# Cross-attention and feed-forward block: the denominators move into the second bank of the tile of the weighted sums

## The chip, the cores and the metric

The kernel runs on one core of one Trainium2 chip. The metric is the device time of one execution in microseconds (us); three runs of the kernel before gave a median of 1290.35 us (1289.89 to 1291.47).

A core has five engines that run beside each other, each with its own queue of instructions that it takes in order: TensorE (PE; its weight loads stand apart as PEld), VectorE (DVE), ScalarE (ACT), GpSimd (POOL) and SyncE (SP), which here issues DMAs. They wait for one another through semaphores. TensorE writes its results to PSUM, where VectorE and ScalarE read them. PSUM has eight banks; a bank holds 512 fp32 numbers in each of 128 partitions.

## The reference

One sequence of 2048 rows of 256 numbers attends to a context of 1601 rows of 192 numbers (and one learned null key and value, so 1602 keys), with 16 heads of 64, and then passes through three layers whose weights are +1 or -1. All in fp32. Cut to what matters:

```python
x = layernorm(x)*g                     # 2048 x 256
q = x @ Wq                             # 16 heads of 64
k, v = split(context @ Wkv); null key and value put in front
sim  = q k^T / 8                       # 2048 x 1602 for each head
attn = softmax(sim)                    # exp(sim - max) / sum
out  = attn @ v                        # the weighted sums, then divided
x = x + layernorm(out @ Wout)*g_out
x = x + three layers(layernorm(x))     # relu between them
```

## The kernel before, in words

**Units.** The attention goes over 32 units `(p, b)`: eight pairs `p` of heads, and for each pair four blocks `b` of 512 rows. The two heads of a pair lie in the two halves of the 128 partitions. The order of all instructions in this part is the order in which the program is written (`manual_schedule`); waits and semaphores are put in by the framework, from what each instruction reads and writes of each tile.

**One unit**, from its scores on, has two stages on TensorE:

- *Scores and the next unit's maxima* (13 steps `k` over the keys, 128 keys each). In step `k` TensorE multiplies keys and queries (`scores`, L391) into one of two tiles `sT`, the even steps into one and the odd steps into the other; ScalarE takes the exponential of it (`exps`, L417) into a tile `e` in SBUF; TensorE then computes one part of the scores of the *next* unit in a cheaper number format (`max_chunk`, L361, and once L345), and VectorE reduces this to maxima (L364, and once L348). In the order of steps L345 with L348 is the last but one and L361 with L364 the last. After the 13 steps VectorE combines the maxima (`max_combined`, L369). GpSimd meanwhile adds the 13 tiles `e` up to `acc` (L665, L667), whose column sums are the denominators of the softmax.
- *Weighted sums.* First the denominators of the *previous* unit: `denominators` (L443) multiplies the previous `acc` by ones with four matmuls on 32 columns of the array each, so that the 512 denominators of each of the two heads stand in 128 partitions by 256 numbers; `divided_quarters` takes the reciprocal of them on VectorE (L455), spreads it with eight copies on ScalarE (L461) and multiplies the previous weighted sums by it on VectorE (L462), which gives `aoT`. Then 13 steps of `weighted` (L424) accumulate values times `e` into bank 0 of the tile `av`; ScalarE copies it to `avs` (L721). After it TensorE transposes the maxima (`max_turned`, L374, read by VectorE in L376), projects the previous unit's `aoT` (`project_out`, L432, added up by VectorE in L437), and makes the queries of the unit after the next (`project_q`, L213) and a part of the next pair's keys or values (`project_k`, `project_v`).

In four units it is otherwise: unit 0 has no previous one, and units 1, 30 and 31 compute the denominators with `divided` (L468) after the third step of the weighted sums. So 28 units go by `denominators` and `divided_quarters`.

**PSUM.** All tiles of PSUM in this part have two banks, `[128, 2, 512]` fp32, and there are four slots of them in two pools of two slots. `flex` gives tiles of the one pool: the tiles of the maxima, `den` (the denominators), `mt` (the transposed maxima), `psq` (queries), and `psk` or `psv` (keys or values). `spare` gives tiles of the other: the two `sT`, `av` and `po` (the projection). A slot is taken over by a new tile when all that read and wrote the old tile is done. `av` uses its bank 0 alone; of a `den` tile 256 numbers of bank 0 are used.

**Two further places** that the prediction looks at. `input_turned` (L491 to L502) transposes the normed input on TensorE: for the blocks 0 and 2 into two PSUM tiles, for block 3 into the two banks of one; ScalarE scales the first half (L498), VectorE the second (L502). `third` (L797 to L825), for the last rows of the third layer, has 32 matmuls (L806), the first sixteen into bank 0 and the others into bank 1 of one tile, and VectorE reads first bank 0 and then bank 1 (L819).

Of the kernel before, what the change touches and what calls it, by code (L numbers as in the profile page):

```python
# [36 lines left out]
def xattn_ffn(ctx, tc, x, ctxT, mask, g_norm, null_kv, wq, wkv, wout, g_out, k0, k1, k2, s0, s1, s2, out):  # L37
# [9 lines left out]
    def flex(name):  # L47
        return ps_f.tile([128, 2, 512], F32, tag="f", name=name)

    def spare(name):  # L50
        return ps_s.tile([128, 2, 512], F32, tag="s", name=name)
# [94 lines left out]
    with ExitStack() as att:  # L146
# [292 lines left out]
        def denominators(acc, ps):  # L439

            for h in range(2):
                for j in range(2):
                    nc.tensor.matmul(  # L443
                        ps[ds(64 * j + 32 * h, 32), :],
                        ones[:, :32],
                        acc[:, j, ts(h, 256)],
                        start=True,
                        stop=True,
                        tile_position=(0, 64 * j + 32 * h),
                    )  # L450

        def divided_quarters(p, b, avs, ps):

            r = lp.tile([128, 256], F32, tag="r", name=f"r_{p}_{b}", bufs=1)
            nc.vector.reciprocal(r, ps)  # L455
            aoT = lp.tile([128, 512], F32, tag="aoT", name=f"aoT_{p}_{b}", bufs=1)

            for j in range(2):
                for h in range(2):
                    for rows in range(2):  # L460
                        nc.scalar.copy(aoT[ds(64 * j + 32 * rows, 32), ts(h, 256)], r[ds(64 * j + 32 * h, 32), :])  # L461
            nc.vector.tensor_tensor(aoT, avs, aoT, ALU.mult)  # L462
            return aoT
# [160 lines left out]
        with tc.manual_schedule():  # L624
            for u, (p, b) in enumerate(units):
# [63 lines left out]


                quarters = last is not None and u not in (1, len(units) - 2, len(units) - 1)
                if quarters:
                    den = flex(f"den_{p}_{b}")[:, 0, :256]
                    denominators(last[3], den)
                    aoT = divided_quarters(*last[:3], den)
                av = spare(f"av_{p}_{b}")
                for k in range(KC):
                    weighted(p, k, es[k], av)
                    if k == 2 and not quarters and last is not None:
# [193 lines left out]
```

## Time and profile before

| | before |
|---|---|
| median of three runs | 1290.35 us |
| span of the profiled execution, first to last instruction | 1288.7 us |
| TensorE busy | 1275.8 us (99%) |
| weight loads on TensorE busy | 648.9 us |
| GpSimd busy | 1001.7 us (78%) |
| VectorE busy | 787.9 us (61%) |
| ScalarE busy | 717.7 us (56%) |
| L391 matmuls of scores, 1664 | 448.5 us |
| L424 matmuls of weighted sums, 1664 | 364.7 us |
| L361 matmuls of maxima, 768 | 276.8 us |
| L443 matmuls of denominators, 224 | 28 groups of 8, 0.64 us each |
| L455 reciprocal, 28 | 1.748 us each |
| mean granted clock of TensorE | 1.000 |

The profile was taken from one execution; its span is what the runs' times are to be compared with. A line of the timeline gives the start and the duration of a group of like instructions in us, its engine and line, what it writes and reads, the shape, and in brackets how long the engine had been idle before it and what ended that. The chain of waits is followed back from the last instruction, at each step to what released it, and so tells which engine and line set the end. Matmuls overlap, and their ends are modelled, so the busy time of TensorE says more of being occupied than of being fast; the distance between starts is the better measure.

### The profile page before, as it was taken

What the parts mean: (1) busy time and instruction counts of PE and PEld (TensorE: products, weight loads), DVE (VectorE), ACT (ScalarE), POOL (GpSimd) and SP (SyncE); (2) the same over time, 40 slices, a digit from 0 to 9 for tenths busy, and PEclk for the clock granted to TensorE, in tenths of its full rate; (3) what the DMA queues carried; (4) which work ended last, traced back from release to release, by engine and by line L of the source; (5) the groups of instructions that cost most, each with busy time, mean ns of one, the idle gap of its engine ahead of it and who ended that gap; (6) DMA issues with size and microseconds to landing.
All of it is one profiled execution on the core that took longest, in us unless ns stands there. A gap on an engine that the chain in (4) does not pass through costs nothing.

```text
span 1288.7 us, 16385 instructions
## 1 busy us (share of the span) xinstructions
PE 1275.8 (99%) x6672; PEld 648.9 (50%) x6672; DVE 787.9 (61%) x817; ACT 717.7 (56%) x965; POOL 1001.7 (78%) x508
## 2 busy tenths in 40 slices
PE   8999999999999999999999999999999999999998
PEld 6334444444444444444444444444444443788887
DVE  7887866655665566556666666666666784644432
ACT  4766556655555555555565666666655667422120
POOL 5798988998889888989899889988998999801100
PEclk9999999999999999999999999999999999999999
DMA  5000000000000000000000000000000010000000
GB/s 145 22 1 5 1 1 13 5 1 1 13 5 2 1 13 5 1 1 13 5 1 1 1 14 5 1 1 5 1 17 1 1 41 1 1 9 9 17 17 17
DMA packets 16156, 13.19 MB, mean 10 GB/s; under 512 B 2688, under 2 KB 15552, under 8 KB 16080
## 3 DMA queue, kind: packets, MB, share of 16 engines
q1 hardware_dynamic: 14944, 11.02, 3.1%
q8 instruction: 52, 0.85, 0.3%
q10 hardware_dynamic: 656, 0.79, 0.2%
q0 software_dynamic: 480, 0.34, 0.2%
q14 instruction: 24, 0.20, 0.1%
HBM read 10.04 MB, written 2.10 MB: 9 GB/s over the span
## 4 chain that ended last, share of the span: by engine, by line
PE 96%; DVE 2%; DMA 1%; ACT 1%; issue 0%; SPq 0%; DVEq 0%; ACTq 0%
PE sT L391 29%; PE av L424 27%; PE ps L775 11%; PE max L361 7%; PE po L432 4%; PE psq L213 4%; PE ps L806 2%; PE psv L303 2%; PE psk L243 1%; PE sT L415 1%; PE den L443 1%; PE psv L315 1%; DMA x_sb<-in_x 1%; PE psk L248 1%; PE max L345 1%; ACT e L417 1%
## 5 line engine op out<-in xcount | busy, mean ns | idle before, releaser
L667 POOL TENSOR_TENSOR acc<-acc,e 128x1024 f32<-128x1024 f32 (+1 forms) x352 | 847.3, 2407 | 27.6
L364 DVE TENSOR_REDUCE mx<-max 128x2 f32<-128x1024 f32 x384 | 450.3, 1220 | 80.3 <-PE max L361 78.4
L417 ACT ACTIVATE e<-sT,maskb 128x1024 f32<-128x1024 f32 (+1 forms) x416 | 460.4, 1113 | 40.4 <-PE sT L391 9.1
L391 PE MATMUL sT<-qT,kT 64*128 64x512 f32 (+1 forms) x1664 | 448.5, 613 | 1.5 <-ACT e L417 0.9
L424 PE MATMUL av<-e,v 128*64 128x512 f32 (+1 forms) x1664 | 364.7, 594 | 0.2 <-ACT e L417 0.2
L361 PE MATMUL max<-kr,qr 64*128 64x512 f32 x768 | 276.8, 712 | 1.9 <-DVE mx L364 1.9
L424 PEld LDWEIGHTS av<-e,v 128*64 128x64 f32 (+1 forms) x1664 | 116.7, 137 | 233.5 <-issue 230.5
L391 PEld LDWEIGHTS sT<-qT,kT 64*128 64x128 f32 (+1 forms) x1664 | 128.2, 181 | 146.6 <-ACT e L417 133.3
L461 ACT COPY aoT<-r 32x256 f32<-32x256 f32 x224 | 90.1, 402 | 63.9 <-DVE r L455 61.6
L361 PEld LDWEIGHTS max<-kr,qr 64*128 64x128 f32 x768 | 75.3, 187 | 95.8 <-DVE mx L364 67.4
L665 POOL TENSOR_TENSOR acc<-e,e 128x1024 f32<-128x1024 f32 x32 | 75.6, 2361 | 61.4 <-ACT seen L655 52.2
L721 ACT COPY avs<-av 128x512 f32<-128x512 f32 x32 | 18.7, 585 | 159.7 <-PE av L424 159.7
L462 DVE TENSOR_TENSOR aoT<-avs,aoT 128x512 f32<-128x512 f32 x28 | 43.1, 1539 | 94.3 <-ACT aoT L461 94.3
L376 DVE TENSOR_TENSOR mT<-mt,pick 128x512 fp32r<-128x512 f32 x32 | 22.1, 689 | 106.9 <-PE mt L374 106.9
L775 PE MATMUL ps<-h0hi,w 128*128 128x512 f32 x256 | 79.5, 392 | 0.0
L775 PE MATMUL ps<-h0lo,w 128*128 128x512 f32 x256 | 78.9, 389 | 0.0
L122 POOL TENSOR_TENSOR y_sb<-y_sb,gout_sb 128x256 f32<-128x256 f32 x12 | 9.3, 775 | 86.7 <-DVE y_sb L89 86.7
L214 ACT ACTIVATE qr<-psq 128x512 fp32r<-128x512 f32 x32 | 19.1, 597 | 97.8 <-PE psq L213 95.1
L763 ACT ACTIVATE h1hi<-ps 128x1024 fp32r<-128x1024 f32 x16 | 16.4, 1026 | 98.9 <-PE ps L775 98.9
L764 DVE SCALAR_TENSOR_TENSOR h1lo<-ps,h1hi 128x1024 fp32r<-128x1024 f32 x16 | 19.6, 1223 | 67.8 <-ACT h1hi L763 67.8
L432 PE MATMUL po<-wo,aoT 128*128 128x256 f32 x256 | 60.6, 379 | 0.0
L213 PE MATMUL psq<-xnT,wq 128*128 128x512 f32 x124 | 58.4, 593 | 0.6 <-ACT xnT L498 0.6
(164 smaller groups left out, 1135.4 us busy)
## 6 DMA issues: line engine op xcount, KB each, us to landing
out_x<-o SPq DMA_DIRECT2D x7, 256.0 KB, 2.2
x_sb<-in_x SPq DMA_DIRECT2D x3, 512.0 KB, 8.2
wa<-in_wkv SPq DMA_DIRECT2D x8, 128.0 KB, 2.7
wq<-in_wq SPq DMA_DIRECT2D x8, 128.0 KB, 2.2
wo<-in_wout SPq DMA_DIRECT2D x8, 128.0 KB, 2.0
xnT<-in_k SPq DMA_DIRECT2D x1, 1024.0 KB, 5.7
wb<-in_wkv SPq DMA_DIRECT2D x15, 64.0 KB, 2.4
ctx_a<-in_ctxT SPq DMA_DIRECT2D x2, 256.0 KB, 8.1
```

Of the source, the lines that this page charges most:

```text
L213: nc.tensor.matmul(ps[:, 0, :], weights[p][0][:, c, :], xnT[:, b, c, :], start=c == 0, stop=c == 1)
L361: nc.tensor.matmul(ps[:, j, :w], qr[rows, ts(t, 128)], kr[rows, ds(start, w)], start=True, stop=True)
L364: nc.vector.tensor_reduce(maxima[p, b][:, t, :, c], ps[:, :, :w], AX.X, ALU.max)
L391: nc.tensor.matmul(ps[:n, j, :], kT[rows, ds(128 * k, n)], qT[rows, :], start=k < 2, stop=k >= 2, skip_group_check=k >= 2,)
L417: nc.scalar.activation(e[:n], ps[:n], AF.Exp, bias=maskb[:n, k : k + 1])
L424: nc.tensor.matmul(av[ts(j, DH), 0, :], v[:n, k, ts(j, DH)], e[:n, j, :], start=k == 0, stop=k == KC - 1)
L432: nc.tensor.matmul(pv[:, t, :], aoT[:, ts(t, 128)], weights[p][3], start=True, stop=True)
L461: nc.scalar.copy(aoT[ds(64 * j + 32 * rows, 32), ts(h, 256)], r[ds(64 * j + 32 * h, 32), :])
L462: nc.vector.tensor_tensor(aoT, avs, aoT, ALU.mult)
L665: nc.gpsimd.tensor_tensor(acc, es[0], es[1], ALU.add)
L667: nc.gpsimd.tensor_tensor(acc[:m], acc[:m], es[k][:m], ALU.add)
L775: nc.tensor.matmul(ps[:, f, :], w(c)[:, ts(2 * g + f, 128)], parts[part][:, c, :], start=i == 0, stop=i == len(steps) - 1,)
```

## The change

The tile `av` is taken from `spare` ahead of the denominators instead of behind them. In the 28 units that go by `denominators`, the four matmuls of L443 write the first 256 numbers of bank 1 of `av`, and the reciprocal (L455) reads them there. No tile `den` is taken from `flex` in these units. Nothing else is changed: the instructions of every engine and their order are as they were, and `divided` in the other units still takes its own tile from `flex`.

```diff
                 quarters = last is not None and u not in (1, len(units) - 2, len(units) - 1)
+                av = spare(f"av_{p}_{b}")
                 if quarters:
-                    den = flex(f"den_{p}_{b}")[:, 0, :256]
+                    den = av[:, 1, :256]
                     denominators(last[3], den)
                     aoT = divided_quarters(*last[:3], den)
-                av = spare(f"av_{p}_{b}")
                 for k in range(KC):
                     weighted(p, k, es[k], av)
                     if k == 2 and not quarters and last is not None:
```

## The prediction

> **What bounds the kernel now.** I read the engines' shares and the chain of waits first, then one unit of the attention loop in order of time, then the list of waits, and last two places far from the change that show how accesses to one PSUM tile are ordered.
>
> ```profile
> span 1288.7 us, 16385 instructions
> ...
> PE 1275.8 (99%) x6672; PEld 648.9 (50%) x6672; DVE 787.9 (61%) x817; ACT 717.7 (56%) x965; POOL 1001.7 (78%) x508
> ...
> PE 96%; DVE 2%; DMA 1%; ACT 1%; issue 0%; SPq 0%; DVEq 0%; ACTq 0%
> ```
>
> TensorE is busy or on the chain nearly throughout: whatever holds it up is paid in full, unless a later wait absorbs it. One unit looks like this at the place of the change (start, duration, engine, line):
>
> ```profile
> 557.41 1.11 ACT L417 ACTIVATE e<-sT,maskb 128x1024 f32<-128x1024 f32 x1
> ...
> 557.77 0.71 DVE L348 TENSOR_REDUCE mx<-max 128x8 f32<-128x528 f32 x1
> ...
> 558.05 0.80 PE L361 MATMUL max<-kr,qr 64*128 64x512 f32 x2
> 558.72 1.11 ACT L417 ACTIVATE e<-sT,maskb 66x1024 f32<-66x1024 f32 x1 [0.20 <-PE sT L391]
> ...
> 558.78 0.64 PE L443 MATMUL den<-acc,ones 128*32 128x256 f32 x8
> 558.89 1.23 DVE L364 TENSOR_REDUCE mx<-max 128x2 f32<-128x1024 f32 x1 [0.41 <-PE max L361]
> ...
> 559.35 3.65 PE L424 MATMUL av<-e,v 128*64 128x512 f32 x16
> ...
> 560.15 0.19 DVE L369 TENSOR_REDUCE mcol<-mx 128x8 f32<-128x32 f32 x1
> 560.25 1.75 DVE L455 RECIPROCAL r<-den 128x256 f32<-128x256 f32 x1
> ```
>
> The weighted sums (L424) start 0.57 us after the denominators (L443), while VectorE has not begun to read these: it first reduces the last maxima (L364) and combines them (L369), and its reciprocal runs from 560.25 to 562.00. Today that reading is off the path, because den has a tile of its own.
>
> **How one PSUM tile is ordered.** The input's transposes stand in two PSUM tiles for block 2 and in the two banks of one tile for block 3. ScalarE reads bank 0 (L498), VectorE bank 1 (L502); everything else is alike.
>
> ```profile
> 64.48 0.69 ACT L498 ACTIVATE xnT<-xT,gn_sb 128x512 f32<-128x512 f32 x1 [0.32 <-PE xT L497]
> 64.58 0.75 DVE L502 TENSOR_SCALAR xnT<-xT,gn_sb 128x512 f32<-128x512 f32 x1 [1.81 <-PE xT L497]
> ...
> 99.92 0.69 ACT L498 ACTIVATE xnT<-xT,gn_sb 128x512 f32<-128x512 f32 x1 [0.43 <-PE xT L497]
> 100.64 0.75 DVE L502 TENSOR_SCALAR xnT<-xT,gn_sb 128x512 f32<-128x512 f32 x1 [2.49 <-ACT xnT L498]
> ```
>
> With two tiles the two reads overlap; with one tile the second starts 0.03 us after the first has ended (100.61), and ACT's L498 is named as its releaser, though the banks differ. The kernel's end says the same of a read behind writes:
>
> ```profile
> 1282.58 0.28 PE L806 MATMUL ps<-w,h1lo 128*128 128x256 f32 x1
> ...
> 1284.50 0.28 PE L806 MATMUL ps<-w,h1lo 128*128 128x256 f32 x1
> 1284.82 0.88 DVE L819 SCALAR_TENSOR_TENSOR o<-ps,s_out,x_sb 128x256 f32<-128x256 f32 x2 [3.08 <-PE ps L806]
> ```
>
> The first L819 reads bank 0 alone, whose sixteen matmuls end with the one at 1282.58 (the next sixteen, 0.12 us apart up to 1284.50, write bank 1). It waits for the last of bank 1, about 2 us too long. So in this program the waits go by tile, not by bank, whatever the chip would allow.
>
> **The change, part by part.**
>
> 1. *den becomes bank 1 of av; the weighted sums write bank 0 of the same tile.* Going by the rows above, the first L424 must now wait for the end of the reciprocal. The instructions on TensorE and VectorE and their order are as before, so the reciprocal cannot move: it follows L364 and L369 in VectorE's queue. It ends at 560.25 + 1.75 = 562.00. A waiting weight load starts about 0.05 us after its releaser's end (the exp that ends at 556.18 is followed by L391's load at 556.23), so L424 starts at 562.05 instead of 559.35: 2.70 us later. Over the 28 units that compute den this way (L455 stands 28 times, and the reciprocal starts 1.47 to 1.48 us after den in each): 28 x 2.70 = **75.6 us**. Bounds: 0, if only the bank counts; 28 x 2.70 otherwise, since neither side of the difference varies by more than 0.01 us.
>
> 2. *What queues behind it.* All 52 L424, then the transpose of the maxima, the projection of the outputs, the next queries and keys or values, and with them the next unit's scores. ScalarE's last exp (to 559.83) and its copies L461 (from 562.03) do not wait for L424; its copy of av (L721) does, and shifts along. Does a later stage absorb it? TensorE's weight loads wait there for exps (133.3 us in all) and for maxima (67.4 us), but these are made in the same stage from scores that shift too: nothing in it was ready early. GpSimd's sums (78% busy) get more room. I take no absorption; at the other end, one that took all would leave 0.
>
> 3. *den's own start.* It waited for the reduction L348 of the tile two back in the rotation (ends 558.48); it will wait for the exp that last read the odd score tile (557.41 + 1.11 = 558.52), from which av takes its slot. That it is this slot is seen today: L424 starts at 559.35, before the other slot's exp ends at 559.83. den started 0.73 us after the last L361 (558.05); in the unit without den, L424 itself starts 0.72 us after its L361 (85.90, 86.62). So TensorE's own finishing and changing over sets this, with some 0.2 us to spare after 558.57: cost 0. Bounds: -15.7 us, all 28 idle times of the weight loads before den; +28 x (559.83 + 0.05 - 558.78) = +31 us, were it the other slot. This overlaps with 1: a later den still ends ahead of the reciprocal's turn unless it passes 560.25, so on top of 75.6 both ends shrink to about nothing.
>
> 4. *The rotation of the maxima is one tile shorter.* The transpose of the maxima takes the slot of the tile read by L348, the queries the slot of the last L364 (read by 560.12) instead of den's. They start at 570.66 and 572.34: more than 10 us of cover, cost 0. The order of all later tiles two apart is unchanged. No DMA and no queue of SP or GpSimd is touched.
>
> Sum: 0 + 75.6 + 0 = 75.6 us on the profiled 1288.7, so a span of 1364.3; the runs' median is 1.65 us above this span: **1366.0 us**.
>
> The Trainium skill ("PSUM — Partial Sum Buffer", section "Summary: rules for kernel authors") speaks for the change: to read PSUM while matmuls run, use another bank and guard by bank. By it the sum would be 0; by the row of L502, 75.6. I go by the row.
>
> **The clock.** Each unit gets a pause of TensorE of 562.05 - 559.42 = 2.63 us, den's end to L424. Two pauses of before enclose it:
>
> ```profile
> 72.90:74.50 1.60, 0.06 (x4) 0.03 (x2) 1.60 (x3) 1.19 (x3) 1.60 (x2) 1.00 0.04 10
> 74.50:78.00 3.50, 3.50 (x20) 1.57 (x20) 3.50 (x4) 2.11 (x2) 3.42 (x2) 1.00 0.00 0
> 1284.80:1287.80 3.00, 0.00 (x0) 0.00 (x0) 0.88 (x2) 0.00 (x0) 0.00 (x0) 1.00 0.26 87
> 1287.90:1288.70 0.80, 0.00 (x0) 0.00 (x0) 0.00 (x0) 0.00 (x0) 0.00 (x0) 0.50 0.00 0
> ```
>
> (columns: length, busy us of PE, PEld, DVE, ACT, POOL, granted clock, DMA.) After 1.54 us without matmuls the clock stayed at 1.00; after the last matmul it still was 1.00 for 3.0 us and then 0.50. At 2.63 us into that idle time it had not fallen, so I take no loss. Upper bound: the run's first matmuls ran at half rate for 5.1 us (24 in 2.70 to 7.80 us, 18 in the 1.9 us from 7.90 on); as much after each pause costs 28 x 5.1 / 2 = 71 us.
>
> The Trainium skill ("TensorE: Matmul & The Clock Gate", section "What's actually happening") has the clock halve after an idle window of about 3.4 us that runs freely; a pause of 2.6 us never fills one, so by it too the loss is 0 unless a mostly idle window counts as idle.
>
> **The rivals.**
> - *Forecast, 0.62:* the wait on the reciprocal at full clock, 1366 (its own range 1362 to 1369).
> - *The wait, and the clock falls in some of the pauses, 0.25:* for it, 2.63 is nearer to 3.0 than to 1.54; against, the clock still stood at 2.63. From 1366 to 1437; with a third of the pauses caught, 1366 + 24 = 1390.
> - *The other side, 0.08:* waits go by bank for a matmul behind a read, which no row of before shows (they show a read behind a read and a read behind writes). Then part 1 is nothing and the time 1290.4. The point that decides is the first L424 of each unit: before or after 562.00 in the unit shown. Were den also freed of all the idle time ahead of it, 1274.7 at the best; 0.01 for that.
> - *Part of the wait is absorbed, 0.04:* for it, 200 us of waits in the stage of the scores; against, part 2. Half absorbed: 1328.
>
> **How the numbers follow.** The likeliest is 1366. The range of 8 in 10 takes all of the forecast and the clock's case up to a third of the pauses: 1362 to 1390; above lies about 0.07, below 0.12. Faster by over 0.2% (what a measurement of this kernel can just tell from none): 0.01; within 0.2%: 0.08; slower: 0.91.
>
> **What would show it.** Right: the list of waits has L424's weight loads behind DVE r L455 some 28 times, 2.6 to 2.7 us each, 75 us in all; L455 still 1.47 us after den; VectorE's L364 and L455 on the chain with some 28 x 3.2 us, 6 to 7%; TensorE at about 93%; a unit 2.70 us longer and the projection later by as much; clock 1.00 at every slice. Wrong: L424 still 0.57 us after den (by bank); slices with a clock below 1.00 and L424 more than 0.43 us apart (clock); den more than 0.73 us behind the last L361 (part 3); a unit longer by less than 2.7 us with L424 late (absorbed).

## The result and the profile after

| | before | after |
|---|---|---|
| median of five runs | 1290.41 us | 1399.28 us |
| span of the profiled execution | 1288.7 us | 1397.6 us |
| mean granted clock of TensorE | 1.000 | 0.974 |
| TensorE busy | 1275.8 us | 1312.0 us |

After takes 1.084 times as long as before (95% interval 1.0829 to 1.0852). The prediction was 1366.0 us with a range of 1362 to 1390: slower, as forecast, but 33 us beyond the forecast and 9 us beyond the range.

The page of after, its engines and its chain of waits by engine:

```profile
span 1397.6 us, 16378 instructions
...
PE 1312.0 (94%) x6672; PEld 657.5 (47%) x6672; DVE 787.1 (56%) x817; ACT 717.3 (51%) x965; POOL 1001.3 (72%) x508
...
PE 91%; DVE 7%; DMA 1%; ACT 1%; issue 0%; SPq 0%; DVEq 0%; ACTq 0%
```

VectorE's share of the chain went from 2 to 7%. The list of waits of after (what waited, for what: us in all, times, longest) names the wait:

```profile
PEld av L424 <- DVE r L455: 87.3, 28, 3.1
...
PE av L424 <- DVE r L455: 73.8, 28, 2.6
```

In before neither line exists. TensorE's matmuls (PE), and not only its weight loads (PEld), stood still 28 times, 73.8 / 28 = 2.64 us each, until the reciprocal was done; the weight loads, which had been idle for longer, 87.3 / 28 = 3.12. The timeline of after at one of these places:

```profile
533.52 0.79 PE L361 MATMUL max<-kr,qr 64*128 64x512 f32 x2
...
534.25 0.64 PE L443 MATMUL av<-acc,ones 128*32 128x256 f32 x8
...
535.72 1.75 DVE L455 RECIPROCAL r<-av 128x256 f32<-128x256 f32 x1
...
537.52 4.06 PE L424 MATMUL av<-e,v 128*64 128x512 f32 x10 [2.64 <-DVE r L455]
```

L443 is still 0.73 us behind L361, the reciprocal still 1.47 us behind L443, and the first L424 is 3.27 us behind L443 instead of 0.57: 2.70 us more, in each of the 28 units between 2.70 and 2.71. That is 28 x 2.706 = 75.8 us. The spans differ by 1397.6 - 1288.7 = 108.9 us, so 33.1 us are something else. The last row hints at it: ten matmuls take 4.06 us, where in before sixteen took 3.65.

The table by windows of after, cut at 459.17 and 534.26 us into pieces of 3.41 us (columns: window, length, busy us of PE, PEld, DVE, ACT and POOL, granted clock, DMA share, GB/s), shows what:

```profile
459.17:462.58 3.41, 1.79 (x16) 0.46 (x14) 2.85 (x5) 2.00 (x2) 3.33 (x2) 1.00 0.00 0
462.58:465.99 3.41, 2.39 (x12) 0.92 (x14) 0.96 (x1) 2.35 (x6) 3.25 (x3) 1.00 0.00 0
534.26:537.67 3.41, 0.77 (x12) 0.29 (x12) 3.08 (x3) 1.22 (x2) 3.25 (x3) 1.00 0.00 0
537.67:541.08 3.41, 3.41 (x10) 0.98 (x10) 0.24 (x1) 3.05 (x8) 3.33 (x2) 0.50 0.00 0
541.08:544.49 3.41, 3.41 (x20) 1.13 (x18) 1.21 (x1) 0.00 (x0) 3.33 (x2) 1.00 0.00 0
```

At 534.26 the window holds the whole pause, TensorE is busy for 0.77 us of it, and in the next window the clock is 0.50 and TensorE begins 10 matmuls instead of 20. At 459.17 the same pause is cut by the window's end, neither window has more than 1.62 us without matmuls, and the clock stays at 1.00.

The whole clock record of after has 21 such stretches at 0.50 in the attention (each is called a fall from here on), each 3.413 us long, and all of them begin and end on one grid of 3.413 us, as if a clock that nothing resets cut time into windows. Ahead of each lies a window with 2.18 us or more without matmuls; the seven pauses that left at most 1.70 us in any one window were not followed by a fall. These are the two windows nearest to each other, each with the one behind it:

```profile
271.43:274.84 3.41, 1.23 (x13) 0.19 (x10) 2.96 (x4) 1.45 (x2) 3.26 (x3) 1.00 0.00 0
274.84:278.26 3.41, 2.95 (x8) 1.00 (x10) 0.40 (x1) 2.89 (x8) 3.33 (x2) 0.50 0.00 0
909.72:913.14 3.41, 1.71 (x16) 0.39 (x12) 2.91 (x4) 1.93 (x2) 3.34 (x2) 1.00 0.00 0
913.14:916.55 3.41, 2.48 (x12) 0.92 (x14) 0.88 (x1) 2.43 (x7) 3.26 (x3) 1.00 0.00 0
```

33.1 / 21 = 1.58 us for a fall, close to the 1.71 that half speed over 3.41 us can cost. In units with a fall the projection (L432) comes 1.4 to 1.7 us later than in units without. The mean clock agrees: 21 x 3.413 x 0.5 / 1397.6 = 0.026 under 1.

The page's row of the clock in 40 slices prints 9 ("90% or more") in every slice, in after as in before: a slice is 35 us long, and one fall takes 5% from it. The prediction wanted to read the clock from these slices; they are too coarse for this, and only the mean clock or short windows show it.

### The profile page after: what moved, and what is told of

It is laid out like the page before. It is cut to its first block, busy times and chain, and to the rows that moved or that the text cites. A ratio compares the mean times of both kernels' runs of the same rounds, so it can differ in the third digit from the quotient of the medians.

```text
span 1397.6 us, 16378 instructions
## 1 busy us (share of the span) xinstructions
PE 1312.0 (94%) x6672; PEld 657.5 (47%) x6672; DVE 787.1 (56%) x817; ACT 717.3 (51%) x965; POOL 1001.3 (72%) x508
## 4 chain that ended last, share of the span: by engine, by line
PE 91%; DVE 7%; DMA 1%; ACT 1%; issue 0%; SPq 0%; DVEq 0%; ACTq 0%
PE av L424 29%; PE sT L391 27%; PE ps L775 10%; PE max L361 6%; PE po L432 4%; PE psq L213 4%; DVE r L455 3%; DVE mx L364 3%; PE ps L806 2%; PE psv L303 1%; PE psk L243 1%; PE sT L415 1%; PE psv L315 1%; DMA x_sb<-in_x 1%; PE psk L248 1%; PE max L345 1%
## 5 line engine op out<-in xcount | busy, mean ns | idle before, releaser
L424 PE MATMUL av<-e,v 128*64 128x512 f32 (+1 forms) x1664 | 399.2, 640 | 74.0 <-DVE r L455 73.8
L424 PEld LDWEIGHTS av<-e,v 128*64 128x64 f32 (+1 forms) x1664 | 124.2, 147 | 336.3 <-issue 245.9
L361 PE MATMUL max<-kr,qr 64*128 64x512 f32 x768 | 277.2, 712 | 2.3 <-DVE mx L364 2.3
L665 POOL TENSOR_TENSOR acc<-e,e 128x1024 f32<-128x1024 f32 x32 | 75.6, 2362 | 91.7 <-ACT seen L655 82.5
L361 PEld LDWEIGHTS max<-kr,qr 64*128 64x128 f32 x768 | 75.5, 187 | 96.0 <-DVE mx L364 68.0
L462 DVE TENSOR_TENSOR aoT<-avs,aoT 128x512 f32<-128x512 f32 x28 | 42.0, 1500 | 94.2 <-ACT aoT L461 94.2
L266 POOL TENSOR_TENSOR kT<-kT 128x256 f32<-128x256 f32 (+1 forms) x48 | 31.8, 662 | 46.9 <-DVE kr L255 43.7
L432 PE MATMUL po<-wo,aoT 128*128 128x256 f32 x256 | 60.6, 379 | 0.0
```

The costliest lines, as they stand in the source:

```text
L361: nc.tensor.matmul(ps[:, j, :w], qr[rows, ts(t, 128)], kr[rows, ds(start, w)], start=True, stop=True)
L424: nc.tensor.matmul(av[ts(j, DH), 0, :], v[:n, k, ts(j, DH)], e[:n, j, :], start=k == 0, stop=k == KC - 1)
L432: nc.tensor.matmul(pv[:, t, :], aoT[:, ts(t, 128)], weights[p][3], start=True, stop=True)
L665: nc.gpsimd.tensor_tensor(acc, es[0], es[1], ALU.add)
```

## The experiments

Times are medians of four to ten runs, each against before on the same chip; e8 has a single run. The headings have the labels (e4 and so on) by which the runs are named further down.

**The pause filled (e4, from after).** Between den and the weighted sums:

```diff
+                    fill = flex(f"fill_{p}_{b}")
+                    for _ in range(3):
+                        nc.tensor.matmul(fill[:, 0, :], ident, es[0][:, 0, :], start=True, stop=True)
```

> The kernel after, with three matmuls on 512 columns (0.86 us each by the 512-column matmuls of L424 and L361 at 0.22 to 0.43 us per half-array pair; an estimate of 2.56 us in all) between den and the weighted sums, whose result nobody reads. They stand in TensorE's pause of 2.63 us and so cost nothing there, and the first L424 still waits for the end of L455, 3.28 us after den. Theory (33 of the 109 us are the clock, which falls to 0.50 for 3.41 us after 21 of the 28 pauses because TensorE has too little to do in them): granted clock 1.000 instead of 0.974, no stretch at 0.50 inside the attention, 1290.4 + 75.8 = 1366 us. Rival (the 33 us are something else that a unit loses behind the wait, and the clock record only goes with it): no faster than after, 1399 us or more.

Measured: 1366.76 us, ratio 1.0596 (1.058 to 1.0612), clock 1.000. The cores' view and the timeline of this kernel:

```profile
core 0: 1364.2 us, clock 1.000
```

```profile
556.07 0.64 PE L443 MATMUL av<-acc,ones 128*32 128x256 f32 x8
...
556.64 2.84 PE L698 MATMUL fill<-e,ident 128*128 128x512 f32 x6
...
557.55 1.75 DVE L455 RECIPROCAL r<-av 128x256 f32<-128x256 f32 x1
...
559.41 1.94 PE L424 MATMUL av<-e,v 128*64 128x512 f32 x8
```

TensorE does more work, L424 starts 0.07 us later than in after (3.34 us behind den), and the kernel is 32.5 us shorter. What the fill changes is that TensorE has no pause; that a tile `fill` is taken from `flex` and a matmul is added has no part in the gain, since e7 below does both and gains nothing. So the 33 us are the clock, and what remains, 1364.2 - 1288.7 = 75.5 us in the spans, is the wait. The theory held, the rival fell.

**One fill matmul instead of three (e6, from after).** `range(1)` in the same edit.

> The kernel after, with one matmul of 512 columns (0.86 us) in TensorE's pause, whose result nobody reads: 2.63 - 0.86 = 1.8 us of the pause are left, in one piece. In after, windows of 3.41 us with at most 1.70 us without matmuls never lowered the clock and those with 2.18 us or more always did; 1.8 us lies between. Theory (a share of a window decides): if the threshold is above 1.8 us, clock 1.000 and 1366 us; if it is at half of a window (1.71 us), only windows that take nearly all of the pause fall, about half of 28, and with 33 us for 21 falls that is 1366 + 22 = 1388 us. Rival (the number of falls does not depend on how long the pause is): 21 falls, 1399 us.

Measured: 1365.01 us, ratio 1.0582 (1.0564 to 1.0599), clock 1.000. The cores' view and the waits of this kernel:

```profile
core 0: 1363.4 us, clock 1.000
```

```profile
PE av L424 <- DVE r L455: 44.3, 28, 1.6
```

The fill took more of the pause than I had reckoned, 1.1 us, so 1.58 us were left, under the 1.70 that had been harmless. No fall in 28 pauses: the number of falls depends on how long the pause is. 1.1 us of fill did as well as 2.8. Here L424 still stands and waits for the reciprocal in all 28 units, and the span is 1363.4 - 1288.7 = 74.7 us over before's: the price of the wait alone, with no fall.

**A short touch in the middle of the pause (e7, from after).**

```diff
+                    if nxt is not None:
+                        fill = flex(f"fill_{p}_{b}")
+                        nc.tensor.matmul(fill[:, 0, :8], ident, mcol[:, :8], start=True, stop=True)
```

> The kernel after, with one short matmul (8 columns) that reads the combined maxima and so stands in the middle of TensorE's pause, where L369 ends (about 1.56 us after den's start): the pause of 2.63 us becomes two, of about 1.0 and 1.6 us, with hardly any work between them. The first L424 still waits for the reciprocal, so 1366 us without any loss of clock. Theory (what counts is how much of a window of 3.41 us TensorE is idle, however it is cut: 2.5 of 3.41 us is over the 2.18 from which the clock of after always fell): granted clock about 0.975 and some 20 stretches at 0.50, 1390 to 1400 us. Rival (what counts is the longest stretch without work; 1.6 us is below the 1.70 at which the clock of after never fell): clock 1.000, 1366 us.

Measured: 1398.65 us, ratio 1.0844 (1.0828 to 1.086), clock 0.976, 20 falls in the attention. Timeline and windows of this kernel at one place:

```profile
532.18 0.64 PE L443 MATMUL av<-acc,ones 128*32 128x256 f32 x8
...
533.88 0.36 PE L699 MATMUL fill<-mcol,ident 128*128 128x8 f32 x2 [1.06 <-DVE mcol L369]
...
535.45 4.92 PE L424 MATMUL av<-e,v 128*64 128x512 f32 x14 [1.21 <-DVE r L455]
```

```profile
532.19:535.60 3.41, 1.14 (x14) 0.59 (x14) 3.08 (x3) 1.22 (x2) 3.25 (x3) 1.00 0.00 0
535.60:539.01 3.41, 3.41 (x10) 0.97 (x10) 0.24 (x1) 3.05 (x8) 3.33 (x2) 0.50 0.00 0
```

Neither of the two idle stretches (1.06 and 1.21 us) is as long as those that did no harm in one piece, and the clock falls all the same. It is the sum of idle time in a window that counts, not the longest stretch: the rival fell. The least idle time ahead of a fall is 1.81 us here, with the touch counted as 0.36 us of work; without it, it would be 2.17, about as in after.

**Half of the reciprocal, first try (e3, from after).**

```diff
-            nc.vector.reciprocal(r, ps)
+            nc.vector.reciprocal(r[:, :128], ps[:, :128])
+            nc.gpsimd.memset(r[:, 128:], 1.0)
```

> The kernel after, where the reciprocal takes 128 of the 256 columns only and the others are set to 1.0 by GpSimd, so half of the denominators are left out. L455 then takes about half of 1.75 us, 0.88. Theory (L424 waits for the end of L455 and for nothing else): first L424 at 1.47 + 0.88 + 0.06 = 2.41 us after den instead of 3.28, so 28 x 1.84 = 51.5 us over before, 1342 us at full clock, and up to 22 us more if half of the pauses, now 1.8 us long, lower the clock. Rival (it waits for something else in VectorE's or ScalarE's queue, such as the copies L461): first L424 still 3.28 us after den, 1366 us or more.

Measured: 1637.24 us, ratio 1.2692 (1.2673 to 1.2711), clock 0.922: more than 270 us above what was expected. The timeline of one unit:

```profile
617.72 26.74 POOL L668 TENSOR_TENSOR acc<-acc,e 128x1024 f32<-128x1024 f32 x11
...
627.19 0.64 PE L443 MATMUL av<-acc,ones 128*32 128x256 f32 x8
...
628.66 0.95 DVE L455 RECIPROCAL r<-av 128x128 f32<-128x128 f32 x1
...
629.66 11.38 PE L424 MATMUL av<-e,v 128*64 128x512 f32 x52 [1.84 <-DVE r L455]
...
644.40 0.20 POOL L456 MEMSET r<- 128x128 f32 x1
644.64 3.29 ACT L462 COPY aoT<-r 32x256 f32<-32x256 f32 x8 [16.40 <-POOL r L456]
```

What was to be measured came out nearly as expected: L424 2.47 us behind den (2.41 expected), after a reciprocal of 0.95 (0.88). But the memset of 0.20 us stands in GpSimd's queue behind the unit's sums (L668), which end at 644.46; the copies L462 need it, wait 16.40 us, and everything behind them is late; with longer pauses of TensorE the clock falls further as well (0.922). I had put a small instruction into the queue that is furthest behind, on the way to something that TensorE needs, and had not asked what stands in front of it.

**Half of the reciprocal, used twice (e3b, from after).**

```diff
-            r = lp.tile([128, 256], F32, tag="r", name=f"r_{p}_{b}", bufs=1)
-            nc.vector.reciprocal(r, ps)
+            r = lp.tile([128, 1, 128], F32, tag="r", name=f"r_{p}_{b}", bufs=1)
+            nc.vector.reciprocal(r[:, 0, :], ps[:, :128])
...
-                        nc.scalar.copy(aoT[ds(64 * j + 32 * rows, 32), ts(h, 256)], r[ds(64 * j + 32 * h, 32), :])
+                        nc.scalar.copy(
+                            aoT[ds(64 * j + 32 * rows, 32), ts(h, 256)].rearrange("p (t q) -> p t q", t=2),
+                            r[ds(64 * j + 32 * h, 32), 0:1, :].to_broadcast([32, 2, 128]),
+                        )
```

> The kernel after, where the reciprocal takes 128 of the 256 columns only and its result is used for both halves, so half of the denominators are left out; nothing is put into GpSimd's queue. Theory (L424 waits for the end of L455 and for nothing else): L455 takes 0.95 us as in the run before, the first L424 comes 1.47 + 0.95 + 0.06 = 2.48 us after den instead of 3.28, so the unit is 1.91 us longer than before's: 28 x 1.91 = 53 us, 1343 us at full clock. The pause is then 1.84 us; the runs so far lowered the clock after a window of 3.41 us with 1.82 us or more without matmuls and not after one with 1.71 or less, so at most the windows that hold the whole of a pause can lower it, half of 28 by chance, up to 22 us more: 1343 to 1365 us, by the number of falls. Rival (L424 waits for something behind the reciprocal, the copies or the sums): first L424 3.28 us after den, 1366 us or more.

Measured: 1361.18 us, ratio 1.0549 (1.0532 to 1.0567), clock 0.986, 11 falls. L424 stands 2.47 to 2.48 us behind den in all 28 units: it waits for the end of the reciprocal and for nothing else. 28 x (2.476 - 0.569) = 53.4 us of the 1359.0 - 1288.7 = 70.3 between the spans are the wait; the other 16.9 are 1.54 us for each of 11 falls. So a smaller wait costs less than in proportion: the pause is shorter, and fewer windows fall. Two places of this kernel by windows:

```profile
841.04:844.45 3.41, 1.57 (x16) 0.48 (x14) 2.66 (x4) 1.81 (x3) 3.32 (x2) 1.00 0.02 5
844.45:847.86 3.41, 3.41 (x10) 0.98 (x8) 0.34 (x1) 2.95 (x8) 3.27 (x2) 0.50 0.00 0
660.14:663.55 3.41, 1.57 (x16) 0.38 (x12) 2.88 (x4) 1.81 (x3) 3.33 (x2) 1.00 0.03 7
663.55:666.96 3.41, 3.41 (x16) 1.17 (x18) 0.13 (x1) 3.17 (x8) 3.25 (x3) 1.00 0.00 0
```

Both first windows hold the whole pause of 1.84 us and have the same 1.57 us of busy TensorE; one is followed by a fall, the other not. Of the 20 windows of this kind 11 fell: those where the pause begins 0.66 to 1.46 us after the window's start, and none of those where it begins up to 0.47 or from 1.55 us on. So the limit lies about here, a little over half of a window, and something else then decides: where in the window the pause stands, which work fills the rest, or how its modelled ends overstate it. Which of these it is stays open.

**den in a tile of its own from the other pool (e5, from before).**

```diff
-                    den = flex(f"den_{p}_{b}")[:, 0, :256]
+                    den = spare(f"den_{p}_{b}")[:, 0, :256]
```

> The kernel before, with den in a tile of its own, but taken from the pool spare, the one from which av comes, instead of flex. Theory (waits go by tile): L424 does not wait for the reciprocal. But av now takes the slot of the other score tile, whose last exp ends 1.05 us after den's start (559.83 to 558.78), so the first L424 comes 1.11 instead of 0.57 us after den: 28 x 0.54 = 15 us, 1305 us, the clock 1.000 since the pause is about 0.5 us long. Rival (what costs is that den lies in the pool of av and sT, not that it shares av's tile): the first L424 still some 3.28 us after den, 1366 to 1399 us.

Measured: 1304.40 us, ratio 1.0115 (1.01 to 1.013), no fall in the attention. Timeline:

```profile
565.92 0.64 PE L443 MATMUL den<-acc,ones 128*32 128x256 f32 x8
...
567.02 1.51 PE L424 MATMUL av<-e,v 128*64 128x512 f32 x6 [0.47 <-ACT e L417]
...
567.39 1.75 DVE L455 RECIPROCAL r<-den 128x256 f32<-128x256 f32 x1
```

L424 starts 0.37 us ahead of the reciprocal that it waited for in after, 1.10 us behind den, and what it waits for is the exp that last read its slot. 28 x 0.54 = 15 us, as expected. Taking den from `spare` costs 14 us by itself; the 109 us need the same tile.

**den in a tile whose other bank is written late (e1, from before).** den in bank 1 of `mt`, with the rotation as in after:

```diff
-                    den = flex(f"den_{p}_{b}")[:, 0, :256]
+                    mt = flex(f"mt_{nxt[0]}_{nxt[1]}")
+                    den = mt[:, 1, :256]
...
-                    max_turned(*nxt)
+                    max_turned(*nxt, mt)
```

> The kernel before, with den in bank 1 of the tile mt (the transposed maxima), whose bank 0 is written about 12 us after den. This shares a tile as after does, and the rotation of the maxima is one tile shorter just as in after, but the neighbour in the tile comes late. Theory (a wait by tile costs only what it is late: the reciprocal ends 3.2 us after den, long ahead of mt's matmul): first L424 0.57 us after den, L374 where it was, 1290 us, same. Rival (the shorter rotation, or the second bank as a place for den, has a part in the 109 us): slower than 1293 us, with den more than 0.73 us behind the last L361 or the queries late.

Measured: 1289.95 us, ratio 1.0001 (0.9991 to 1.001). Timeline (lines one further on than in before):

```profile
155.55 0.64 PE L444 MATMUL mt<-acc,ones 128*32 128x256 f32 x8
...
156.12 4.08 PE L425 MATMUL av<-e,v 128*64 128x512 f32 x18
...
157.02 1.75 DVE L456 RECIPROCAL r<-mt 128x256 f32<-128x256 f32 x1
```

Sharing a tile costs nothing where the neighbour's first write comes after the reader is done, and the shorter rotation of `flex`, which after has too, costs nothing either.

**av taken early, den left in flex (e2, from before).** The line `av = spare(...)` moved up, as in the change, and nothing else.

> The kernel before, with av only taken from its pool ahead of the denominators; den stays a tile of flex. Theory: the place where av is taken has no instruction of its own and changes no order, so 1290.4 us, same, L424 0.57 us after den. Rival (the early taking ties the denominators to av's slot): slower.

Measured: 1289.72 us, ratio 1.0001 (0.9991 to 1.001); L424 0.57 us behind den. The place of the line has no cost of its own.

**Two tiles at the kernel's end (e8, from before).** This tries the rule from which the prediction came, at the place where it was read:

```diff
+            two = [ps, ps]
+            if b == NB - 1 and g == 1:
+                two[1] = slot(f"ps2_{b}_{g}_1")
...
-                                ps[:, j, :D],
+                                two[j][:, j, :D],
...
-                        o[:, j, :], ps[:, j, :D], s_out, x_sb[:, t, :], ALU.mult, ALU.add
+                        o[:, j, :], two[j][:, j, :D], s_out, x_sb[:, t, :], ALU.mult, ALU.add
```

> The kernel before, where the last rows of the third layer go into two tiles of PSUM instead of the two banks of one; nothing else is changed. Theory (waits go by tile, not by bank): the first L819 starts when the sixteenth of the last matmuls is done, at about 1282.9 us of before's time scale, 2 us ahead of the end of the last matmul, instead of 0.04 us after it; the time gains at most 0.4 us, which cannot be measured. Rival (waits go by bank, and L819 was late for another reason): L819 starts where it did.

Measured: 1289.39 us in one run, which says nothing of 0.4 us. The timeline (L819 is L822 here, L806 is L809):

```profile
1281.93 0.28 PE L809 MATMUL ps<-w,h1lo 128*128 128x256 f32 x1
...
1282.25 0.48 DVE L822 SCALAR_TENSOR_TENSOR o<-ps,s_out,x_sb 128x256 f32<-128x256 f32 x1 [1.17 <-PE ps L809]
...
1283.85 0.28 PE L809 MATMUL ps<-w,h1lo 128*128 128x256 f32 x1
```

The sixteenth of the last matmuls starts at 1281.93, and the first read now follows it, 1.6 us ahead of the last matmul's start. In before it stood 0.32 us behind the start of the last one, at 1284.50. Two tiles part what two banks of one tile did not.

No run has den in av's tile and leaves out the wait, so none shows what the chip itself does when one bank of a tile is read while the other is written. For banks of two tiles before shows it: the reciprocal reads den from 560.25 to 562.00 while L424, from 559.35 on, writes av, and it takes 1.75 us, as it does in after, where TensorE stands still. So what is shown is that the program's waits tell tiles apart and not banks; that the chip would need the wait is not shown, and these lines speak against it.

## Why the prediction was right and wrong

*Part 1, the wait.* Right to the size: 2.706 us in each of 28 units, 75.8 us against 75.6. Without falls the span is 75.5 (e4) and 74.7 us (e6) over before's. The rows of L502 and L819, from which the rule "by tile" was taken, stood far from the change and showed no matmul behind a read; that the rule holds for this too was an extrapolation, and it came true. e8 showed the rule at work at one of these rows, e5 and e1 at the place of the change itself.

*Part 2, nothing absorbed.* Right: in units without a fall the projection L432 comes 14.75 us behind den instead of 12.05, 2.70 later. The line of before belongs to the den at 558.78 in the prediction; the other two are from after:

```profile
570.83 1.89 PE L432 MATMUL po<-wo,aoT 128*128 128x256 f32 x8
```

```profile
310.26 0.64 PE L443 MATMUL av<-acc,ones 128*32 128x256 f32 x8
...
325.01 1.89 PE L432 MATMUL po<-wo,aoT 128*128 128x256 f32 x8
```

*Parts 3 and 4.* Right: L443 stays 0.72 to 0.73 us behind L361; the shorter rotation costs nothing (e1).

*The clock.* This is the step that failed, in these words: "At 2.63 us into that idle time it had not fallen, so I take no loss." It was taken at 0 and measured 33 us: 21 falls of 1.58 us. The observation was true and the inference was not. It took the end of the run as showing a delay, counted from the last matmul, that a pause has to outlast. What the end of before showed, cut on its grid, is this:

```profile
1284.44:1287.85 3.41, 0.34 (x3) 0.13 (x2) 0.88 (x2) 0.00 (x0) 0.00 (x0) 1.00 0.23 77
1287.85:1288.70 0.85, 0.00 (x0) 0.00 (x0) 0.00 (x0) 0.00 (x0) 0.00 (x0) 0.50 0.00 0
```

The clock did not fall because 3.0 us had passed; it fell at the end of a window that had been mostly idle, though not wholly: TensorE was busy for its first 0.34 us. A pause of 2.63 us spoils such a window just as well, and pays afterwards, when the matmuls are back. The rival "the clock falls in some of the pauses" had the case right, with a chance of 0.25, but not its sizes. For the top of the range it took a third of the pauses at 5.1 / 2 = 2.55 us each, 24 us; measured were three quarters of them at 1.58 us, 33 us. The 5.1 us were read from the rate of the run's first matmuls, over more than one window; a fall in after lasted one. The share was too low, the price too high, and the two errors partly cancel.

How often it happens can be estimated. With windows of W = 3.41 us that stand anywhere against a pause of L, some window loses at least T of its time for W + L - 2T of every W positions. With T = 1.84 from e3b, a pause of 2.64 us gives (3.41 + 2.64 - 3.68) / 3.41 = 0.70, some 19 or 20 of 28, against 21 measured; a pause of 1.84 gives 0.46, 13 of 28, against 11; the 1.58 of e6 and the 1.54 in before give none. This is a fit and no forecast, and that it comes so near is in part luck. T comes from a later run; in e3b not 13 but 20 pauses lay whole in a window, and 11 of these were followed by a fall. Nor do the pauses stand anywhere: a fall delays the next pause and so sets where it stands on the grid. In after, from the seventh pause to the 26th, three falls follow each other and one pause goes without, over and over; den of every fourth unit starts at 496.43, 646.58, 796.75 and 946.89, 150.1 to 150.2 us apart, and 44 windows of 3.413 us are 150.2. The three quarters are the share of this pattern.

The Trainium skill ("TensorE: Matmul & The Clock Gate", section "What's actually happening") has a window of 3413 ns that runs freely; the grid of 3.413 us in these records agrees. It says that the clock halves after an idle window. These runs differ on what idle means: windows with TensorE busy for 1.57 of 3.41 us lowered it (e3b). The prediction named that reading ("unless a mostly idle window counts as idle") and did not follow it into the sum.

## What to carry to other kernels

A pause of a busy TensorE is to be priced twice: its length, and the half-speed window behind it, here 1.5 to 1.6 us in a share of the pauses that depends on their length and on where they fall on the grid (21 of 28 pauses of 2.64 us, 11 of 28 of 1.84, none of 28 of 1.58); below some 1.6 us of idle time in a window the second price was nil, and matmuls in the pause, whose result nobody reads, removed it (33 us here) though the wait itself stayed. Two banks of one tile were one object to this program's waits: before a tile is shared, find the first access to its other bank and see whether it comes before or after the reader is done (12 us later cost nothing, 0.57 us later cost 109 us). An instruction moved or added to an engine's queue comes when that queue reaches it: 0.20 us on GpSimd cost 276 us (1637.24 in e3 against 1361.18 in e3b), what the clock lost by the longer pauses included.

## What was not expected of the hardware

- The granted clock changed only on a grid of 3.413 us that no pause shifted, and each fall in the attention of after lasted exactly one window.
- A window did not have to be idle: 2.18 us or more without matmuls in 3.41 lowered the clock each time in after, up to 1.70 never, 1.84 in 11 of 20 windows of e3b.
- A matmul of 8 columns in the middle of the pause did not keep the clock up (1398.65 us); 1.1 us of matmuls did (1365.01 us).
